# Selective scan and first attention: every third product with b on GpSimd, the second direction's convolution on TensorE, its softplus on GpSimd, and attention values as the stationary operand

## The chip, the cores and the metric

The kernel runs on one core of a Trainium2 chip. It is one launch that holds a whole network of twelve blocks. The metric is the device time in microseconds, lower is better; times are medians of several runs, and each profile is one profiled execution of its own.

## The reference, cut to what matters

The input x has 4 sequences of 128 tokens and 128 channels, the context has 4 sequences of 2048 rows and 96 columns. Twelve blocks are added to x one after the other. The change touches the first two.

The first block is an attention with ternary weights and 8-bit activations. Keys and values are the same projection of the image features, 64 wide and written twice side by side:

```python
for Wa, ba in ((W_att0, b_att0), (W_att1, b_att1)):
    kv = bitnet_linear(image_embeds, Wa, ba)
    k = jnp.concatenate([kv, kv], axis=-1)
    scores = jnp.einsum('bse,bpe->bsp', fused, k) * inv_sqrt_e
    attn = jax.nn.softmax(scores, axis=-1)
    fused = fused + 0.1 * jnp.einsum('bsp,bpe->bse', attn, k)
```

So there are two rounds, each over 4 sequences, 128 queries against 2048 keys.

The second block runs a selective scan over the tokens in both directions and adds the two. For each direction, with 256 inner channels and 16 states:

```python
xc = silu(causal_depthwise_conv4(xi) + conv_b)
delta = softplus(dt @ dtp_w.T + dtp_b)
# for each token t:
dA = jnp.exp(d_t[:, :, None] * A)
h = h * dA + (d_t * u_t)[:, :, None] * b_t[:, None, :]
y = jnp.einsum('bdn,bn->bd', h, c_t)
```

## The kernel before, in words

Tokens of all four sequences lie side by side: 512 columns, and channels lie on the 128 partitions. The code is written as a flow of tile operations, each with its engine named; a framework sets the semaphores and fixes the order of each engine's queue before the run. That order is near the order in the code but not the same: an instruction that is ready is let past one that is not. In the trace the second half of a unit's score matmuls (L959) stands ahead of the transpose o_tr (L996), which the code has first. On the chip each queue is then run in order.

**First attention**, `bit_attention`. A unit is one round and one sequence, so there are eight. The keys kT (L924) and the values v (L931) of a round are in one tile kv; v has 16 chunks of 128 keys for each sequence, 65 wide, and the 65th column is 1 (memset on GpSimd, L910). A unit makes queries (L946 to L949: a matmul with the folding matrix `fold`, a scaling, and the bias added to fused), scores in two groups of 16 matmuls (L959) into PSUM tiles of 1024 columns of which there are three, the maximum over the keys (L961, L964), a transpose, a second maximum, a transpose that spreads it, and a copy (L966 to L973). Then weights: the maximum is subtracted (L977, VectorE) and the exponential taken (L979, ScalarE), one tile p for each group, out of three. Last, values: 32 matmuls (L988) with p as the stationary operand (128 columns) and v as the moving one (65 columns); the 65th output column is the sum of weights. VectorE takes its reciprocal (L992), scales and doubles the 64 columns to 128 (L994), TensorE transposes (L996) and VectorE adds to fused (L997). The values of unit i-1 are written in the code after the weights of unit i. At i = 2 two more ternary weights are made on VectorE (L840, L841, tiles of the tag qtmp, which has two buffers); at i = 3 and 4 half of the context's mask each is loaded by a DMA of SyncE (L1024) into a qtmp tile and turned into floats on GpSimd (L1027).

**Selective scan**, `mamba`. After a layernorm (its square is on GpSimd, L341) `setup(d)` prepares direction d: input projection, a padded copy (L1160 on GpSimd for the zeros, L1161 on ScalarE), the convolution as one product and three fused products and sums on VectorE for each half of the channels (L1165, L1167), silu, projections for dt, b and c, `softplus` for each half (L1084 to L1101, ScalarE for Abs, Exp and Ln, VectorE for the rest), and du (L1205). `setup(0)` runs first; `setup(1)` is a generator that is advanced one step for each state n of direction 0.

Then for each of the 16 states n: b and c are spread over the partitions by a matmul with a one-hot stationary operand (L1210) into PSUM tiles of the tag mm, of which there are three; c is copied to SBUF (cs, L1223, ScalarE), VectorE multiplies du with b (dbu, L1225, 128x1024), and for each half ScalarE takes the exponential dA (L1231, three PSUM tiles in turn) and VectorE runs the scan h (L1234). GpSimd multiplies h with c (hc, L1237, 128x1024) and TensorE adds hc into y with an identity as stationary operand (L1239). The tiles cs, dbu, h and hc have three buffers each. At the end y is gated (L1247, L1249) and projected (L1255).

Both operands of GpSimd's product lie in SBUF, which is what the copy of c is for; b is read by VectorE straight from PSUM.

Of the kernel before, what the change touches and what calls it, by code (L numbers as in the profile page):

```python
# [9 lines left out]
F32 = mybir.dt.float32  # L10
# [4 lines left out]
ALU = mybir.AluOpType  # L15
# [3 lines left out]
P = 128  # L19
B = 4  # L20
T = 128
C = 128
N = B * T
S = 2048
NS = B * S
DC = 96
NCH = S // P
# [233 lines left out]
def bc_mid(ap, n):  # L261

    return ap.unsqueeze(1).to_broadcast([ap.shape[0], n, ap.shape[1]])
# [7 lines left out]
class Net:  # L271
# [534 lines left out]
    def bit_attention(self, nxt):  # L806


        nc, tc = self.nc, self.tc
        w = self.load("l0x")  # L810
        with ExitStack() as es:
            one = es.enter_context(tc.tile_pool(name="bit1", bufs=1))
            wk = es.enter_context(tc.tile_pool(name="bit2", bufs=2))
            big = es.enter_context(tc.tile_pool(name="bit_big", bufs=2))
            BIG = NS // 2 + B * NCH * 65
            qp = es.enter_context(tc.tile_pool(name="bit_q", bufs=1))
            tp = es.enter_context(tc.tile_pool(name="bit_t", bufs=3))

# [30 lines left out]
            ps = es.enter_context(tc.tile_pool(name="bit_ps", bufs=2, space=PSUM))  # L849
# [4 lines left out]
            s, inv = self.absmax([self.ctxT[:DC, b * S : b * S + S] for b in range(B)], "am_ctx")  # L854
# [20 lines left out]
            s, inv = self.absmax(stretches(vis), "am_vis")  # L875
# [3 lines left out]
            total = one.tile([P, NS // W], F32, name="total")  # L879
# [10 lines left out]
            s, inv = self.absmax([xT], "am_x")  # L890
# [11 lines left out]
            fold = one.tile([P, 2, 64], F32, name="fold")  # L902
# [3 lines left out]
            for r, n in enumerate(("att0", "att1")):  # L906
                kv = big.tile([P, BIG], F32, tag="big", name="kv")
                kT = kv[:, 0 : NS // 2]
                v = kv[:, NS // 2 :].rearrange("p (c w) -> p c w", w=65)
                nc.gpsimd.memset(v[:, :, 64:65], 1.0)  # L910
                osc = out_scale(n, s_img)
                osc10 = self.small(1, "osc10" + n)
                nc.vector.tensor_scalar_mul(osc10, osc, 0.1)
                rounds.append((n, kT, v, osc10))
                pairs = qimg.rearrange("p (c h k) -> p c h k", h=2, k=P)
                for j in range(B):
                    mm = stp.tile([P, W], F32, tag="st", name="k_ps")
                    for lo in range(0, W, 512):
                        at = (j * W + lo) // P
                        for h in range(2):  # L920
                            nc.tensor.matmul(
                                mm[h * 64 : h * 64 + 64, lo : lo + 512], qw[:, L0X[n]], pairs[:, at : at + 4, h],
                                start=True, stop=True)
                    nc.scalar.activation(  # L924
                        kT[:, j * W : j * W + W], mm, AF.Identity, bias=self.col("b_" + n), scale=osc)
                    mm = stp.tile([P, W], F32, tag="st", name="v_ps")
                    for i in range(NCH):
                        at = (j * NCH + i) * P
                        nc.tensor.matmul(
                            mm[:, i * 64 : i * 64 + 64], qimg[:, at : at + P], qw[:, L0X[n]], start=True, stop=True)  # L930
                    nc.vector.tensor_copy(  # L931
                        v[:, j * NCH : j * NCH + NCH, 0:64], mm.rearrange("p (c w) -> p c w", w=64))

            class Unit:

# [8 lines left out]
                def queries(u):  # L944
                    mm = ps.tile([P, 512], F32, tag="mm", name="fq_ps")
                    nc.tensor.matmul(mm[:, 0:T], self.flat(fold), u.fb, start=True, stop=True)  # L946
                    u.q = wk.tile([P, T], F32, tag="fq", name="fq")
                    nc.vector.tensor_scalar_mul(u.q, mm[:, 0:T], 1.0 / math.sqrt(C))
                    nc.vector.scalar_tensor_tensor(  # L949
                        u.fb, self.col("b_" + u.n).to_broadcast([P, T]), 0.1, u.fb, ALU.mult, ALU.add)  # L950
                    u.mh = wk.tile([P, 2, P], F32, tag="mh", name="mh")

                def scores(u, g):
                    u.st[g] = stp.tile([P, 2, HC // 2, P], F32, tag="st", name="st")
# [20 lines left out]
                def weights(u, g):  # L975
# [3 lines left out]
                    nc.scalar.activation(p, p, AF.Exp)  # L979
                    u.ts.append(p)  # L980

                def values(u):
                    av = ps.tile([P, 512], F32, tag="mm", name="av")
                    for g in range(2):
                        for h in range(2):
                            for c in range(HC // 2):
                                ch = u.b * NCH + 2 * (g * (HC // 2) + c) + h
                                nc.tensor.matmul(  # L988
                                    av[:, 0:65], u.ts[g][:, h * (HC // 2) + c], u.v[:, ch],
                                    start=g + h + c == 0, stop=g + h == 2 and c == HC // 2 - 1)  # L990
                    r = self.small(1, "rsum")
                    nc.vector.reciprocal(r, av[:, 64:65])  # L992
                    o = wk.tile([P, 2, 64], F32, tag="o", name="o")
                    nc.vector.tensor_scalar(o, bc_mid(av[:, 0:64], 2), r, u.osc10, ALU.mult, ALU.mult)  # L994
                    mm = ps.tile([P, 512], F32, tag="mm", name="o_tr")
                    nc.tensor.transpose(mm[:, 0:P], self.flat(o), self.ident)  # L996
                    nc.vector.tensor_add(u.fb, u.fb, mm[:, 0:P])  # L997

            units = [Unit(r, b) for r in range(2) for b in range(B)]
            units[0].queries()  # L1000
# [80 lines left out]
        nc.gpsimd.memset(self.ctx[:, :, DC : DC + 1], 1.0)  # L1081
        nc.sync.dma_start(self.ctx[:, :, 0:DC], self.A["ctx"].rearrange("(c p) d -> p c d", p=P))

    def softplus(self, pool, out, v, bias, w):  # L1084

        nc = self.nc
        e = pool.tile([P, w], F32, tag="sp_e", name="sp_e")
        nc.scalar.activation(e, v, AF.Abs, bias=bias)  # L1090
        nc.scalar.activation(e, e, AF.Exp, scale=-1.0)
        s = pool.tile([P, w], F32, tag="sp_s", name="sp_s")
        nc.vector.tensor_scalar_add(s, e, 1.0)
        ln = pool.tile([P, w], F32, tag="sp_l", name="sp_l")
        nc.scalar.activation(ln, s, AF.Ln)
        r = pool.tile([P, w], F32, tag="sp_r", name="sp_r")
        nc.vector.tensor_scalar(r, v, bias, 0.0, ALU.add, ALU.max)
        nc.vector.tensor_scalar_add(s, s, -1.0)
        nc.vector.tensor_sub(e, e, s)
        nc.vector.tensor_add(ln, ln, e)  # L1100
        nc.vector.tensor_add(out, r, ln)  # L1101

    def mamba(self, nxt):

# [7 lines left out]
        with ExitStack() as es:  # L1112
# [22 lines left out]
            xn = one.tile([P, B, C], F32, name="xn")  # L1135
            self.layernorm(tp, self.x, xn)
            yT = one.tile([P, 2, 2, N], F32, name="yT")

            def mm_tile(name):
                return ps.tile([P, N], F32, tag="mm", name=name)  # L1140

            def setup(d):
# [12 lines left out]
                for half in range(2):  # L1155
                    i = d * 2 + half
                    mm = mm_tile("xi_ps")
                    nc.tensor.matmul(mm, w[:, at + half * P : at + half * P + P], xT, start=True, stop=True)
                    pad = tp.tile([P, B, T + 3], F32, tag="pad", name="pad")
                    nc.gpsimd.memset(pad[:, :, 0:3], 0.0)  # L1160
                    nc.scalar.copy(pad[:, :, 3:], mm.rearrange("p (b t) -> p b t", b=B))  # L1161
                    yield
                    cw = self.col("conv_w")[:, i * 4 : i * 4 + 4]
                    acc = tp.tile([P, B, T], F32, tag="conv", name="conv")
                    nc.vector.tensor_scalar_mul(acc, pad[:, :, 0:T], cw[:, 0:1])  # L1165
                    for k in range(1, 4):
                        nc.vector.scalar_tensor_tensor(  # L1167
                            acc, pad[:, :, k : k + T], cw[:, k : k + 1], acc, ALU.mult, ALU.add)
                    nc.scalar.activation(
                        u[:, half], self.flat(acc), AF.Silu, bias=self.col("conv_b")[:, i : i + 1])  # L1170
                    yield
# [24 lines left out]
                for half in range(2):  # L1196
                    i = d * 2 + half
                    mm = mm_tile("dt_ps")
                    nc.tensor.matmul(
                        mm, dtp[96:XP, d * 256 + half * P : d * 256 + half * P + P], dt[96:XP],  # L1200
                        start=True, stop=True)
                    self.softplus(tp, delta[:, half], mm, self.col("dtp_b")[:, i : i + 1], N)
                    yield
                du = wk.tile([P, 2, N], F32, tag="du", name="du")
                nc.vector.tensor_mul(du, delta, u)  # L1205
# [9 lines left out]
            for d in range(2):  # L1215
# [3 lines left out]
                for n in range(16):  # L1219
# [2 lines left out]
                    cs = lp.tile([P, N], F32, tag="cs", name="cs")  # L1222
                    nc.scalar.copy(cs, cn)  # L1223
                    dbu = lp.tile([P, 2, N], F32, tag="dbu", name="dbu")
                    nc.vector.tensor_mul(dbu, du, bc_mid(bn, 2))  # L1225
                    h = lp.tile([P, 2, N], F32, tag="h", name="h")
                    for half in range(2):
                        j = (d * 2 + half) * 16 + n
# [741 lines left out]
```

## Time and profile before

| | |
|---|---|
| median of 3 runs | 1679.18 us (1677.23 to 1680.57) |
| the profiled execution | 1656.7 us |
| its span, first to last instruction | 1654.5 us |
| mean granted TensorE clock | 0.824 |
| busy: PE, DVE, ACT, POOL | 1228.3, 999.1, 620.6, 140.9 us |
| first attention's units (window) | 80 to 170 us |
| states of the scan, both directions | 228 to 372.7 us |

PE is TensorE's matmuls and PEld its loads of the stationary operand, DVE is VectorE, ACT is ScalarE, POOL is GpSimd, SP is SyncE. A line of the chain of work gives start, length and what ran; "issue" is time in which the engine waited for nothing that the profile shows. A line of waits reads: who waited, for whom, us in total, times, longest. A line in order of time reads: start, length, engine, line, operation, output<-inputs, shapes, and in brackets how long the engine had been idle and what ended that. A group line reads: count | busy us, mean ns | idle before. Where several instructions are merged (x2), the length is that of all.

### The profile page before, as it was taken

Reading aid. Unit: us, or ns where it says so; the run is one execution under the profiler, and the core shown is the slowest. Engines: PE = TensorE matmul, PEld = TensorE weight load, DVE = VectorE, ACT = ScalarE, POOL = GpSimd, SP = SyncE. Lnnn points to the kernel's source line nnn. Section 1 sums busy time; section 2 is a strip of 40 time slices with the busy share of each in tenths; the row PEclk is TensorE's granted clock in tenths of the full one; section 3 lists DMA queues with packets and bytes.
Section 4 is the critical chain, followed back from the end, with each engine's and each line's share of the span. In section 5 each row is a group of like instructions: output and inputs, shape, how many; then the busy total and the mean of one; then the engine's idle time right before and its main releaser. Section 6 shows DMA issues by size and latency. Waiting matters only on the chain.

```text
span 1654.5 us, 15539 instructions
## 1 busy us (share of the span) xinstructions
PE 1228.3 (74%) x6142; PEld 656.7 (40%) x6142; DVE 999.1 (60%) x1568; ACT 620.6 (38%) x796; POOL 140.9 (9%) x108
## 2 busy tenths in 40 slices
PE   2688456676999999999648054989958148899857
PEld 0377222224444444444213032754426024555534
DVE  8966478993266767667567954124657665444335
ACT  3722255442155655556333001324523102333332
POOL 0010024470000000000002000000020100000000
PEclk9967558798599999999869576978978567899778
DMA  5000000005000000000010004010000000000010
GB/s 158 1 1 1 0 0 26 0 1 161 1 24 1 0 1 1 0 1 1 0 51 1 0 0 127 1 23 19 1 2 1 9 0 1 1 2 1 7 48 7
DMA packets 9371, 28.19 MB, mean 17 GB/s; under 512 B 1175, under 2 KB 7104, under 8 KB 8142
## 3 DMA queue, kind: packets, MB, share of 16 engines
q1 hardware_dynamic: 8174, 24.88, 5.2%
q10 hardware_dynamic: 1120, 2.27, 0.4%
q8 instruction: 50, 0.82, 0.2%
q14 instruction: 27, 0.22, 0.0%
HBM read 26.88 MB, written 0.26 MB: 16 GB/s over the span
## 4 chain that ended last, share of the span: by engine, by line
PE 62%; DVE 25%; ACT 5%; issue 4%; POOL 3%; DMA 1%; POOLq 0%; ACTq 0%; DVEq 0%; SPq 0%
PE sc L495 12%; PE av L529 12%; PE s_ps L673 3%; DVE na_m L678 3%; PE mm L1317 3%; PE t_ps L697 3%; PE q_ps L438 2%; DVE h L1234 2%; PE av L988 2%; PE av L710 2%; PE h_ps L1666 2%; PE y_ps L1673 2%; PE y_ps L1239 2%; POOL hc L1237 1%; PE st L959 1%
## 5 line engine op out<-in xcount | busy, mean ns | idle before, releaser
L495 PE MATMUL sc<-q_aug,ctxT 99*128 99x512 f32 x448 | 213.2, 602 | 1.8 <-DVE q_aug L439 1.8
L529 PE MATMUL av<-s,ctx 128*97 128x512 f32 x448 | 206.8, 597 | 6.6 <-ACT s L527 6.0
L497 ACT COPY s<-sc 128x1024 f32<-128x1024 f32 x112 | 112.9, 1008 | 114.8 <-PE sc L495 114.8
L526 DVE TENSOR_TENSOR s<-s,mbs 128x1024 f32<-128x1024 f32 x112 | 132.4, 1218 | 38.8 <-ACT mbs L521 38.8
L678 DVE TENSOR_REDUCE na_m<-s_ps 128x2 f32<-128x1024 f32 x64 | 75.8, 1221 | 89.8 <-PE s_ps L673 89.6
L527 ACT ACTIVATE s<-s 128x1024 f32<-128x1024 f32 x112 | 115.5, 1056 | 36.0 <-DVE s L526 35.3
L505 DVE TENSOR_TENSOR m<-m,s 128x1024 f32<-128x1024 f32 x72 | 87.9, 1221 | 66.3 <-ACT s L497 66.3
L529 PEld LDWEIGHTS av<-s,ctx 128*97 128x97 f32 x448 | 73.1, 165 | 125.0 <-issue 105.6
L495 PEld LDWEIGHTS sc<-q_aug,ctxT 99*128 99x128 f32 x448 | 82.7, 193 | 93.9 <-issue 82.7
L1239 PE MATMUL y_ps<-hc,consts 128*128 128x512 f32 x128 | 75.3, 723 | 33.6 <-POOL hc L1237 30.7
L703 ACT ACTIVATE p<-t_ps 128x1024 f32<-128x1024 f32 x64 | 62.0, 1021 | 92.5 <-PE t_ps L697 92.5
L1237 POOL TENSOR_TENSOR hc<-h,cs 128x1024 f32<-128x1024 f32 x32 | 77.5, 2433 | 86.3 <-DVE h L1234 86.0
L1234 DVE TENSOR_TENSOR_SCAN h<-dA,dbu 128x512 f32<-128x512 f32 x64 | 74.4, 1202 | 3.6 <-ACT dA L1231 3.4
L341 POOL TENSOR_TENSOR ln_sq<-ln_xc 128x512 f32<-128x512 f32 (+1 forms) x19 | 23.3, 1227 | 503.4 <-DVE ln_xc L339 496.6
L673 PE MATMUL s_ps<-kT,q 32*128 32x512 f32 x256 | 63.7, 711 | 2.1 <-DVE na_m L678 1.1
L697 PE MATMUL t_ps<-q,kT 32*128 32x128 f32 x1024 | 56.3, 329 | 8.8 <-DVE na_m L678 5.8
L1239 PEld LDWEIGHTS y_ps<-hc,consts 128*128 128x128 f32 x128 | 26.0, 222 | 83.2 <-POOL hc L1237 57.0
L697 PEld LDWEIGHTS t_ps<-q,kT 32*128 32x128 f32 x1024 | 46.7, 223 | 27.3 <-DVE na_m L678 16.2
L1231 ACT ACTIVATE dA<-delta,A 128x508 f32<-128x508 f32 x64 | 42.7, 689 | 33.1 <-DVE h L1234 32.1
L358 PE MATMUL tr_xnT<-consts,xn 128*128 128x128 f32 x32 | 8.7, 428 | 60.0 <-DVE xn L348 41.2
L345 ACT ACTIVATE ln_sd<-ln_v,eps 128x4 f32<-128x4 f32 (+1 forms) x19 | 5.7, 300 | 124.5 <-DVE ln_v L343 124.5
L439 DVE TENSOR_SCALAR q_aug<-q_ps,qb 99x512 f32<-99x512 f32 x20 | 15.0, 751 | 46.5 <-PE q_ps L438 46.5
(574 smaller groups left out, 2128.7 us busy)
## 6 DMA issues: line engine op xcount, KB each, us to landing
w_moe<-in_moe SPq DMA_DIRECT2D x2, 2048.0 KB, 8.2
ctxT<-in_ctxT SPq DMA_DIRECT2D x4, 768.0 KB, 12.6
rows<-in_rows ACTq DMA_DIRECT2D x1, 2048.0 KB, 12.4
w_l3f<-in_l3f SPq DMA_DIRECT2D x1, 1920.0 KB, 8.0
w_l0f<-in_l0f SPq DMA_DIRECT2D x1, 1024.0 KB, 4.9
w_mamba<-in_mamba SPq DMA_DIRECT2D x1, 976.0 KB, 19.0
w_r<-in_r SPq DMA_DIRECT2D x1, 960.0 KB
consts<-in_consts SPq DMA_DIRECT2D x1, 832.0 KB, 17.1
```

The source lines that it names most:

```text
L495: nc.tensor.matmul(sc[:, i], self.ctxT[:, at : at + P], u.q, start=True, stop=True)
L497: nc.scalar.copy(s, sc)
L505: nc.vector.tensor_max(u.m, u.m, u.s[j])
L526: nc.vector.tensor_sub(p, p, bc_mid(u.mb, 2))
L527: nc.scalar.activation(p, p, AF.Exp)
L529: nc.tensor.matmul(u.av[: DC + 1], self.ctx[:, u.b * NCH + chunks[2 * j + i]], p[:, i], start=j + i == 0, stop=j == n - 1 and i == 1)
L673: nc.tensor.matmul(ts[g // 2][:, g % 2], qs[lo : lo + 32], kT[lo : lo + 32, s, j * 512 : j * 512 + 512], start=True, stop=True)
L678: nc.vector.tensor_reduce(part[:, at : at + 2], t, axis=AX, op=ALU.max, negate=True)
L697: nc.tensor.matmul(ts[g // 2][:, g % 2, j], kT[g * 32 : g * 32 + 32, s, at : at + P], qs[g * 32 : g * 32 + 32], start=True, stop=True)
L1234: nc.vector.tensor_tensor_scan(h[:, half], self.flat(dA), dbu[:, half], 0.0, ALU.mult, ALU.add)
L1237: nc.gpsimd.tensor_mul(hc, h, bc_mid(cs, 2))
L1239: nc.tensor.matmul(y[:, half], self.ident, hc[:, half], start=n == 0, stop=n == 15)
```

## The change

Every third state's product with b moves to GpSimd, with a copy of b to SBUF on ScalarE. The convolution of the second direction becomes four accumulating matmuls per half with diagonal matrices, which GpSimd makes once from the identity. The five VectorE steps of softplus other than the one that reads PSUM move to GpSimd in the second direction. In the first attention, v becomes the stationary operand (64 columns) and p the moving one (128 columns); even and odd chunks write to the two halves of the output's partitions; the sum of weights is made by three adds on GpSimd for each group and two matmuls with a matrix of ones; the halves are folded by a matmul with `fold`.

```diff
+                half = p[:, 0 : HC // 2]
+                a = wk.tile([P, HC // 2, P], F32, tag="qtmp", name="psum")
+                nc.gpsimd.tensor_add(a, half, p[:, HC // 2 :])
+                nc.gpsimd.tensor_add(a[:, 0:2], a[:, 0:2], a[:, 2:4])
+                nc.gpsimd.tensor_add(u.total[:, g], a[:, 0], a[:, 1])
 def values(u):
     av = ps.tile([P, 512], F32, tag="mm", name="av")
     for g in range(2):
-        for h in range(2):
-            for c in range(HC // 2):
+        for c in range(HC // 2):
+            for h in range(2):
                 ch = u.b * NCH + 2 * (g * (HC // 2) + c) + h
                 nc.tensor.matmul(
-                    av[:, 0:65], u.ts[g][:, h * (HC // 2) + c], u.v[:, ch],
-                    start=g + h + c == 0, stop=g + h == 2 and c == HC // 2 - 1)
-    r = self.small(1, "rsum")
-    nc.vector.reciprocal(r, av[:, 64:65])
-    o = wk.tile([P, 2, 64], F32, tag="o", name="o")
-    nc.vector.tensor_scalar(o, bc_mid(av[:, 0:64], 2), r, u.osc10, ALU.mult, ALU.mult)
-    mm = ps.tile([P, 512], F32, tag="mm", name="o_tr")
-    nc.tensor.transpose(mm[:, 0:P], self.flat(o), self.ident)
-    nc.vector.tensor_add(u.fb, u.fb, mm[:, 0:P])
+                    av[h * 64 : h * 64 + 64, 0:T], u.v[:, ch], u.ts[g][:, h * (HC // 2) + c],
+                    start=g + c == 0, stop=g == 1 and c == HC // 2 - 1)
+    mm = ps.tile([P, 512], F32, tag="mm", name="rsum")
+    for g in range(2):
+        nc.tensor.matmul(mm[:, 0:T], self.ones, u.total[:, g], start=g == 0, stop=g == 1)
+    o = wk.tile([P, T], F32, tag="o", name="o")
+    nc.vector.reciprocal(o, mm[:, 0:T])
+    nc.vector.tensor_mul(o, o, av[:, 0:T])
+    nc.tensor.matmul(mm[:, T : 2 * T], self.flat(fold), o, start=True, stop=True)
+    nc.vector.scalar_tensor_tensor(u.fb, mm[:, T : 2 * T], u.osc10, u.fb, ALU.mult, ALU.add)
...
-    def softplus(self, pool, out, v, bias, w):
+    def softplus(self, pool, out, v, bias, w, eng):
...
-        nc.vector.tensor_scalar_add(s, e, 1.0)
+        eng.tensor_scalar_add(s, e, 1.0)
...
-        nc.vector.tensor_scalar_add(s, s, -1.0)
-        nc.vector.tensor_sub(e, e, s)
-        nc.vector.tensor_add(ln, ln, e)
-        nc.vector.tensor_add(out, r, ln)
+        eng.tensor_scalar_add(s, s, -1.0)
+        eng.tensor_sub(e, e, s)
+        eng.tensor_add(ln, ln, e)
+        eng.tensor_add(out, r, ln)
...
+            diag = one.tile([P, 8, P], F32, name="diag")
+            for j in range(8):
+                nc.gpsimd.tensor_scalar_mul(diag[:, j], self.ident, self.col("conv_w")[:, 8 + j : 9 + j])
...
+                    if d:
+                        acc = mm_tile("conv_ps").rearrange("p (b t) -> p b t", b=B)
+                        for k in range(4):
+                            nc.tensor.matmul(
+                                acc, diag[:, half * 4 + k], pad[:, :, k : k + T], start=k == 0, stop=k == 3)
+                    else:
...
-                    self.softplus(tp, delta[:, half], mm, self.col("dtp_b")[:, i : i + 1], N)
+                    self.softplus(
+                        tp, delta[:, half], mm, self.col("dtp_b")[:, i : i + 1], N, nc.gpsimd if d else nc.vector)
...
-                    nc.vector.tensor_mul(dbu, du, bc_mid(bn, 2))
+                    if n % 3 == 2:
+                        bs = lp.tile([P, N], F32, tag="bs", name="bs", bufs=1)
+                        nc.scalar.copy(bs, bn)
+                        nc.gpsimd.tensor_mul(dbu, du, bc_mid(bs, 2))
+                    else:
+                        nc.vector.tensor_mul(dbu, du, bc_mid(bn, 2))
```

Besides, v loses its 65th column and the memsets that filled it (L910), and each unit gets a tile `total` for the sums.

More of the change, by code (lines that the diff above doesn't have):

```diff
@@ L814, in bit_attention @@
             big = es.enter_context(tc.tile_pool(name="bit_big", bufs=2))
-            BIG = NS // 2 + B * NCH * 65
+            BIG = NS
             qp = es.enter_context(tc.tile_pool(name="bit_q", bufs=1))
@@ L908, in bit_attention @@
                 kT = kv[:, 0 : NS // 2]
-                v = kv[:, NS // 2 :].rearrange("p (c w) -> p c w", w=65)
-                nc.gpsimd.memset(v[:, :, 64:65], 1.0)
+                v = kv[:, NS // 2 :].rearrange("p (c w) -> p c w", w=64)
                 osc = out_scale(n, s_img)
@@ L931, in bit_attention @@
                     nc.vector.tensor_copy(
-                        v[:, j * NCH : j * NCH + NCH, 0:64], mm.rearrange("p (c w) -> p c w", w=64))
+                        v[:, j * NCH : j * NCH + NCH], mm.rearrange("p (c w) -> p c w", w=64))
             class Unit:
@@ L951, in queries @@
                     u.mh = wk.tile([P, 2, P], F32, tag="mh", name="mh")
+                    u.total = wk.tile([P, 2, P], F32, tag="total", name="total")
                 def scores(u, g):
@@ L1163, in setup @@
                     cw = self.col("conv_w")[:, i * 4 : i * 4 + 4]
[L1164 to L1168, printed above, removed]
+                    if d:
[4 more added lines that the diff above has]
+                    else:
+                        acc = tp.tile([P, B, T], F32, tag="conv", name="conv")
+                        nc.vector.tensor_scalar_mul(acc, pad[:, :, 0:T], cw[:, 0:1])
+                        for k in range(1, 4):
+                            nc.vector.scalar_tensor_tensor(
+                                acc, pad[:, :, k : k + T], cw[:, k : k + 1], acc, ALU.mult, ALU.add)
                     nc.scalar.activation(
```

## Prediction

> **What bounds the kernel now.** I read the page's busy tenths and chain first, then the busy time of the two stages that the diff touches, then the chain, the waits and the instructions in order of time inside them. The change lies in the first 382 us; the other 1272 us of the span are the same instructions and I give them no change. By stage (length, busy time of PE, PE loads, DVE, ACT and POOL with counts, granted clock):
>
> ```profile
> 80.00:170.00 90.00, 75.08 (x568) 68.00 (x568) 55.91 (x99) 21.52 (x26) 7.52 (x2) 0.72 0.01 1
> 228.00:372.70 144.70, 99.87 (x211) 36.68 (x210) 133.75 (x128) 73.28 (x112) 77.64 (x33) 0.85 0.02 8
> ```
>
> The scan stretch (228 to 372.7) is bound by DVE: busy 133.75 of 144.7 us, idle 11. POOL works half of it and waits for DVE's scans. In the second direction the chain is DVE alone, 6.72 us for two states n:
>
> ```profile
> 346.53 1.20 DVE dbu L1225 x2
> 347.73 0.97 issue
> 348.86 0.97 issue
> 349.83 1.76 DVE h L1234 x2
> 352.06 1.19 DVE h L1234
> 353.25 1.20 DVE dbu L1225 x2
> ```
>
> The attention (80 to 170) is bound by PE where the clock is low and shared with DVE where it is full. Its waits:
>
> ```profile
> DVE rsum L992 <- PE av L988: 10.1, 5, 5.2
> ACT p L979 <- DVE p L977: 14.3, 9, 1.9
> POOL hc L1237 <- DVE h L1234: 86.0, 23, 26.4
> ACT dA L1231 <- DVE h L1234: 32.1, 22, 3.3
> ```
>
> The last two are of the scan. In time, one unit's value product at the low and one at the full clock, and DVE and POOL together in the scan:
>
> ```profile
> 131.36 6.93 PE L988 MATMUL av<-kv,p 128*128 128x65 f32 x32
> 143.73 3.68 PE L988 MATMUL av<-kv,p 128*128 128x65 f32 x32
> 258.87 2.44 POOL L1237 TENSOR_TENSOR hc<-h,cs 128x1024 f32<-128x1024 f32 x1 [2.95 <-DVE h L1234]
> 259.14 2.72 DVE L1167 SCALAR_TENSOR_TENSOR conv<-pad,cols,conv 128x512 f32<-128x512 f32 x1
> 262.92 0.72 DVE L1167 SCALAR_TENSOR_TENSOR conv<-pad,cols,conv 128x512 f32<-128x512 f32 x1
> ```
>
> The same DVE step takes 2.72 us when a POOL product starts first and 0.72 when POOL is idle.
>
> **What the Trainium skill says.** "SBUF — State Buffer", section "Who interferes with whom": DVE and GpSimd share one pair of ports; a DVE instruction with two SBUF inputs is blocked whole by a GpSimd one that reads SBUF, one with a single SBUF input is not. The trace agrees: 2.72 against 0.72 above, while the scans (one input in PSUM) stay at 1.13 to 1.22 us beside hc. "GPSIMD Engine Reference", section 3.1: an elementwise product of two tensors is 1.96 times slower on GpSimd; here hc takes 2.34 us where dbu, of the same shape, takes 1.16 on DVE: 2.0. "TensorEngine Tiling (Array Packing)", section "When to Use Tiling": with at most 64 columns on the moving side, swap the operands and tile two columns wide. No two-wide 128-row product is in the trace; a four-wide one (L710, 32 matmuls) takes 1.07 us, against 3.68 above. "TensorE: Matmul & The Clock Gate", Part 1: the clock falls to half after idle time; the trace has 0.50 from 102 to 114 us, though PE is 96% busy there, so I don't build on a rule for it.
>
> **The change part by part.**
>
> *Third products (L1225).* n = 2, 5, 8, 11, 14 of each direction, ten in all. Off DVE: 10 x 1.16 = 11.6 us. Onto POOL: 10 x 2.34 (the hc row) = 23.4 us. Onto ACT: ten copies bn to bs at 0.59 (the cs row) = 5.9 us, beside 73 us of work in 145, so hidden; the one bs buffer frees when POOL has done its product. POOL's queue is in order: behind a product stands the next hc, behind that y's matmuls; ahead of it may stand hc of n-1.
>
> *Convolution of direction 2 (L1165, L1167).* Off DVE, with the blocking in them: 1.15+0.72+1.70+0.72 and 0.46+2.72+0.72+0.72 = 8.9 us. Onto PE: 8 matmuls of 128x512, 0.43 us each at full clock, 0.86 at half: 3.4 to 6.9 us. PE is busy 100 of 145 us here, so they are hidden; it takes one of the three mm banks for longer, which I count in the stalls below. The eight diag products on POOL (128x128, one input, no such row; between the 128x128 memset at 0.21 and the 128x128 product at 0.72, so 1.7 to 5.8 us, I take 3.5) come before ln_sq and the pad memset in POOL's queue. POOL is free from 183 to 189, so most is hidden; if they start only with x ready at 185.9, ln_sq, which is on the chain, is late by 0 to 3 us. I take +1.
>
> *Softplus of direction 2 (L1093, L1098 to L1101).* Off DVE: (0.40+0.43+0.67+0.66+1.35) + (0.43+0.40+0.67+1.71+0.66) = 7.4 us. Onto POOL: per half two one-input steps (no row; below the 1.05 of ln_sq on 128x512, above half of it: 0.6) and three at 1.05 = 4.35; 8.7 in all. Its length from input to delta was 8 to 9 us a half on DVE and stays about so; the four states left after setup hide it.
>
> *Sum of the stretch.* DVE 133.75 - 11.6 - 8.9 - 7.4 = 105.9 us. POOL 77.6 + 23.4 + 8.7 = 109.7 us. If nothing is lost, the stretch is 110; if DVE's old idle time stays and POOL costs nothing, 144.7 - 27.9 = 116.8. The unknown is the idle time s that each of the ten POOL products gives to DVE. In steady state POOL has four products in three states, 9.4 us, and DVE 9.2, where it had 3 x 3.36 = 10.1; with three dbu buffers a product can start three states ahead, so s can be near zero; at the worst hc and the product stand one after the other between two scans, 2 x 2.34 + 0.3 = 5. Steps with two SBUF inputs that stay (du, x3, yT, six in all) are blocked for about as long as now. Two engines with equal load cannot both be full: I take s = 1. Stretch 116.8 + 10 = 127, gain 18.
>
> *Attention.* Value product: 32 matmuls now take 3.68 us (115 ns each) at full and 6.93 at half clock, and 3.09+6.73+6.35+6.73+3.52+3.52+5.49 = 35.4 us of them are on the chain. After, 64 columns are loaded for each and 128 stream, in pairs: at best half of a lone 128-column pass (the chain has L495 at 1.72 us for four of 512 columns, 430 ns each; 430/4/2 = 54 ns); at worst the 70 ns of the score pairs (1.16 us for 16, a pair of row halves). I take 62, a ratio of 0.54: -16 us. Two matmuls with ones take 0.3 to 0.5 us more per unit: +3. The reciprocal grows from 128x1 (0.17) to 128x128. The nearest row is
>
> ```profile
> L1368 DVE RECIPROCAL nrm<-nrm 128x512 f32<-128x512 f32 x1 | 3.4, 3352 | 0.0
> ```
>
> so a quarter, 0.84 us; with mul 0.28 for o 0.41 it is +0.54 per unit, on DVE's way between two maxima: +4. The transpose becomes the fold matmul, the add a fused step, same cost. POOL gets three adds per group, 1.05 + 0.84 + 0.70 = 2.6 us, 5.2 per unit in 8 to 12 us: hidden, since values come a unit later. But they run when DVE does mh's max (L964) and the bias step (L949), both with two SBUF inputs and the max on the chain: a block of 0 to 1.05 us, I take 0.4 per unit, +3. The psum tile shares the two qtmp slots with the mask: the mask's DMAs (SP, L1024) wait for a free slot, and behind them on SP the dtp load, needed 80 us later; the mask steps (POOL, L1027, 3.76 us each) stand ahead of the sums of two units: 0 to 3 us, hidden by the unit of slack. The two memsets (L910) were hidden: nothing. Sum -16 + 3 + 4 + 3 = -6, from -13 (no block, no visible reciprocal) to +2 (sums late by 2 to 3 us in two units, PE waiting in order behind).
>
> *Total.* -18 + 1 - 6 = -23 us. The profiled execution took 1656.7 us (span 1654.5 and 2.2 around it), so 1633.7 for such a one; the median of the runs, 1679.18, is 22.5 us above it and the cut is taken off that: 1656.
>
> **The rivals.** With s the time is 1679.2 - 32.9 + 10 s (27.9 and 6 off, 1 on).
>
> *Slower: POOL's product in the scan's path.* If hc(n-1) and then dbu(n) stand between scan n-1 and scan n, s is 5: -32.9 + 50 = +17, 1696 us. It decides from s = 3.3 on. For it: POOL would be 86% busy at 127 us and its order is fixed. Against it: in the trace dbu is made for two states ahead of the scans (1.20 x2, then four h), so the order looks ahead.
>
> *Little gain.* s = 2 and the attention gives nothing (blocks, the reciprocal, clock): -32.9 + 6 + 20 = -7, 1672 us. For it: at full clock a unit is 8.2 us with 6.9 of DVE in it, and DVE gets 0.5 more.
>
> *More gain.* s = 0 and the denser products keep the clock up, so that the low-clock units (12.5 us) go toward 8.2: -33 and some -6 more, 1640 us.
>
> **How the numbers follow.** Forecast 0.58, more gain 0.07, little gain 0.17 (of which 0.07 comes out within 0.2%), slower 0.18. A measurement of this kernel can tell about 0.2%, 3.4 us, from no change. Faster 0.58 + 0.07 + 0.10 = 0.75. The range reaches from just under the best case, 1638, to 1682, where only the slower case is left out.
>
> **What would show it.** Right: the scan stretch at about 127 us with DVE near 106 and POOL near 110 busy; dbu on POOL at 2.3 to 2.5 us; DVE waiting for POOL about 10 us in all; 32 av matmuls in 2.0 us at full clock; a reciprocal of 0.84; mh's max sometimes at 1 us instead of 0.28. Wrong: POOL products longer than 2.6, h waiting for a POOL dbu for over 3 us each, units of attention no shorter than 10 us on average, ln_sq late by more than 3 us, or the stages after 382 us changed in length by more than 5.

## The result and the profile after

The changed kernel takes 1660.89 us (median of 4 runs, 1657.26 to 1665.40), the kernel before beside it 1679.88 us (1677.23 to 1682.20): ratio 0.9889, 95% interval 0.9855 to 0.9923. Ratios here and below leave out executions over 1.5% above the fastest of their kernel, while differences in us are between medians of all, so the two need not agree (in e3 below, 18 and 23 us). The forecast of 1656.0 us was 5 us too low. The sign and the size came out, yet the two terms behind them did not: the scan costs time, and the attention gives far more than its 6 us.

The profiled executions stand the other way round: 1656.7 us before, 1663.99 us after (span 1661.7). The kernel before scatters from 1656 to 1690 us from one execution to the next, and its profile caught a quick one. So I compare stages at fixed marks. The scan's layernorm (ln_sq, L341) starts at 189.42 us before and 184.81 after, the next block's ln_sq at 383.57 and 392.45: the first part is 4.6 us shorter, the scan's block 207.6 instead of 194.2 us. From there to the end it is the same code, 1270.9 and 1269.3 us.

The two stages after the change, as length, busy time of PE, PE loads, DVE, ACT and POOL with counts, and granted clock:

```profile
80.00:163.80 83.80, 61.68 (x627) 50.77 (x627) 66.27 (x104) 22.70 (x28) 46.53 (x50) 0.84 0.01 2
223.30:380.80 157.50, 112.32 (x223) 41.93 (x222) 110.79 (x100) 80.98 (x124) 112.23 (x53) 0.81 0.02 7
```

In the attention the clock is 0.84 instead of 0.72 and TensorE 74% busy instead of 83%. In the scan DVE has 111 us of work instead of 134 and the stretch is 13 us longer: each of DVE and POOL is busy for some 70% of it, and neither alone sets its length. The waits of the scan say where (engine, line, who released it; total, times, longest):

```profile
POOL hc L1261 <- DVE h L1258: 38.5, 16, 6.2
DVE h L1258 <- POOL dbu L1247: 18.8, 9, 4.8
DVE dbu L1249 <- PE b_ps L1229: 13.7, 4, 8.5
DVE du L1224 <- POOL delta L1109: 3.5, 1, 3.5
DVE sp_r L1105 <- POOL delta L1109: 3.3, 1, 3.3
```

The first was there before (86.0 us then). The other four are 39 us in which DVE stands; with the old scan the third is 1.8 us (e3 below) and the rest are not there. The chain in the second direction, which was DVE alone, now runs in this order (pieces under 0.1 us left out):

```profile
343.68 2.35 POOL hc L1261
346.03 2.32 POOL dbu L1247
348.41 1.10 issue
349.51 1.21 DVE h L1258
350.88 2.11 POOL hc L1261
352.99 0.20 issue
353.19 2.35 POOL hc L1261
355.54 2.32 POOL dbu L1247
357.88 1.23 DVE h L1258
```

Two hc, one dbu, and only then the next scan: POOL's product does not start ahead, it is queued behind hc of the states just scanned. The price of the instructions was not the fault:

```profile
L1247 POOL TENSOR_TENSOR dbu<-du,bs 128x1024 f32<-128x1024 f32 x10 | 24.0, 2400 | 23.4 <-DVE du L1224 21.8 <-ACT bs L1246 1.6
L1101 POOL TENSOR_SCALAR sp_s<-sp_e 128x512 f32<-128x512 f32 x2 | 3.2, 1582 | 0.0
L1107 POOL TENSOR_TENSOR sp_e<-sp_e,sp_s 128x512 f32<-128x512 f32 x2 | 2.5, 1266 | 0.2
```

dbu is 2.40 us, as forecast. The steps of softplus are dearer than forecast (1.58 and 1.27 against 0.6 and 1.05). In the attention, one unit's value product, and the reciprocal and the maximum on DVE:

```profile
136.17 1.97 PE L995 MATMUL av<-p,kv 128*64 128x128 f32 x32
```

```profile
L1002 DVE RECIPROCAL o<-rsum 128x128 f32<-128x128 f32 x8 | 7.6, 952 | 5.0 <-PE rsum L1000 5.0
L964 DVE TENSOR_TENSOR mh<-mh 128x128 f32<-128x128 f32 x8 | 4.2, 521 | 0.1
```

The 1.97 us are the 62 ns per matmul of the forecast; the reciprocal takes 0.95 (forecast 0.84); the maximum 0.52 on average, 0.285 before. These 62 ns are for one record of the trace, which has two for each value matmul of the code: the x32 are the 16 value matmuls of a unit. The score matmuls and those of the convolution have two records each as well.

### The profile page after: what moved, and what is told of

It reads as the page before. It is cut to its first block, busy times and chain, and to the rows that moved or that the text cites. A ratio compares the mean times of both kernels' runs of the same rounds, so it can differ in the third digit from the quotient of the medians.

```text
span 1661.7 us, 15727 instructions
## 1 busy us (share of the span) xinstructions
PE 1229.6 (74%) x6198; PEld 645.5 (39%) x6198; DVE 985.0 (59%) x1540; ACT 628.5 (38%) x808; POOL 217.5 (13%) x182
## 4 chain that ended last, share of the span: by engine, by line
PE 61%; DVE 23%; POOL 6%; ACT 5%; issue 4%; DMA 1%; POOLq 0%; ACTq 0%; DVEq 0%
PE sc L495 12%; PE av L529 12%; PE s_ps L673 4%; DVE na_m L678 3%; PE mm L1341 3%; PE t_ps L697 3%; PE q_ps L438 2%; POOL hc L1261 2%; PE h_ps L1690 2%; PE av L710 2%; PE y_ps L1697 2%; PE y_ps L1263 2%; DVE h L1258 2%; PE o_ps L1762 1%; POOL ln_sq L341 1%
## 5 line engine op out<-in xcount | busy, mean ns | idle before, releaser
L1263 PE MATMUL y_ps<-hc,consts 128*128 128x512 f32 x128 | 81.5, 785 | 34.4 <-POOL hc L1261 33.7
L703 ACT ACTIVATE p<-t_ps 128x1024 f32<-128x1024 f32 x64 | 62.0, 1021 | 91.4 <-PE t_ps L697 91.3
L341 POOL TENSOR_TENSOR ln_sq<-ln_xc 128x512 f32<-128x512 f32 (+1 forms) x19 | 23.3, 1226 | 496.0 <-DVE ln_xc L339 496.0
L1258 DVE TENSOR_TENSOR_SCAN h<-dA,dbu 128x512 f32<-128x512 f32 x64 | 74.3, 1207 | 21.3 <-POOL dbu L1247 18.8
## 6 DMA issues: line engine op xcount, KB each, us to landing
rows<-in_rows ACTq DMA_DIRECT2D x1, 2048.0 KB, 13.2
```

What stands on the lines that cost most here:

```text
L1258: nc.vector.tensor_tensor_scan(h[:, half], self.flat(dA), dbu[:, half], 0.0, ALU.mult, ALU.add)
L1263: nc.tensor.matmul(y[:, half], self.ident, hc[:, half], start=n == 0, stop=n == 15)
```

## The experiments

The theory that these runs came to test: the attention gives all of the gain, and by TensorE's clock rather than by its work; the scan's edits cost some 13 us, because POOL's queue holds the next scan back. The clock came into it only after the first four runs, whose expectations do not know of it. The rivals: the scan gains as forecast and the attention little; within the scan, that POOL's load or the convolution's place in TensorE's queue is what costs; for the clock, that it falls by chance.

### The two kernels again, and each half of the change alone

**e1_before_again**: no edit.

> The kernel before, unchanged. Its first profiled execution took 1656.7 us while its timed runs took 1677 to 1682. If the 23 us between them is a property of single executions, this profile and these times should scatter over both values; if it is a property of the chip or of the day, the profile taken here should agree with the times taken here within 0.3%, and its stages should tell where the 23 us lie. In the stages that the diff touches I expect the same lengths as in the first profile: attention units to about 170 us, scan stretch 144.6 us.

Measured: 1678.15 us (1658.38 to 1689.55), ratio to the kernel before 1.0009 (0.9960 to 1.0058).

**e2_after_again**: no edit.

> The changed kernel, unchanged. By its first profile the x of the scan is ready 9 us later than in the first profile of before (390.0 against 381.0 us): attention 7 us shorter, scan stretch 157.5 instead of 144.6 us. Theory A (the profiles compare like with like): about 7 us slower than before on the same chip. Theory B (the prediction: DVE's load decides): 19 to 23 us faster, and the scan stretch is then not what the profile shows.

Measured: 1661.51 us (1657.24 to 1669.72), ratio 0.9927 (0.9905 to 0.9949).

**e3_attention_alone**: `bit_attention` from the change, the scan from the kernel before.

> Only the attention with stationary values; the scan as before. Prediction's term: 6 us faster. By the first profile of the changed kernel: 7 us faster (last values done at 163.6 instead of 170.5 us).

Measured: 1653.02 us (1649.94 to 1660.70), ratio 0.9891 (0.9842 to 0.9939).

**e4_scan_alone**: the other way round.

> Only the three edits of the scan; the attention as before. Prediction's term: 17 us faster, with the scan stretch at about 127 us. By the first profile of the changed kernel (chain hc, then dbu on POOL, then h): scan stretch about 157 us and 13 us slower than before.

Measured: 1691.68 us (1687.38 to 1694.64), ratio 1.0108 (1.0060 to 1.0155).

What follows: the attention alone is 23 us faster than the kernel before (1675.8 us beside it), the scan's edits alone are 16 us slower. e3 is far beyond the 6 to 7 us that were expected, and e2 met neither of its theories: it is 14 us faster, with the long scan of the first profile. The marks give the cost of the scan more exactly, since the same code after them took 1267 to 1280 us in these profiles. The block from ln_sq to ln_sq: 194.2 and 194.8 us in the two profiles of the kernel before and 194.4 in e3, 207.6 and 207.8 in the two of the change, 205.2 in e4. The scan's edits cost 11 to 13 us in their own block. The first part, to the scan's ln_sq: 184.8, 184.2 and 183.3 us with the new attention; 189.4, 211.0 and 211.9 with the old one. So most of the scatter of the kernel before is the old attention's: of the 31 us between its two profiles 22 lie there and 9 in the code after the scan. That a middling execution, of which there is no profile, is slow for the same reason is likely and not shown.

With it goes the clock. Old attention (e4, then the first profile of the kernel before), then the new one (e3); the fields are those of the stages above:

```profile
90.00:100.00 10.00, 10.00 (x65) 9.77 (x63) 3.73 (x6) 1.86 (x3) 0.00 (x0) 0.50 0.00 0
...
120.00:140.00 20.00, 17.50 (x94) 15.53 (x93) 11.59 (x18) 2.68 (x5) 7.51 (x2) 0.50 0.01 3
140.00:160.00 20.00, 19.11 (x107) 17.69 (x106) 8.28 (x14) 4.46 (x5) 0.00 (x0) 0.50 0.00 1
```

```profile
120.00:140.00 20.00, 17.50 (x99) 15.90 (x98) 9.31 (x15) 4.76 (x6) 7.22 (x2) 0.50 0.01 1
140.00:160.00 20.00, 16.31 (x157) 14.35 (x155) 14.66 (x26) 4.95 (x7) 0.00 (x0) 0.98 0.00 1
```

```profile
120.00:140.00 20.00, 15.01 (x148) 12.53 (x148) 16.02 (x24) 5.33 (x7) 17.98 (x15) 0.83 0.01 3
140.00:160.00 20.00, 14.48 (x152) 11.92 (x152) 13.40 (x24) 4.76 (x6) 13.41 (x17) 0.91 0.00 1
```

In e4 the clock is 0.50 while TensorE is 88 to 100% busy. The first profile of the kernel before left this low clock at about 140 us; e4 kept it to the attention's end, and so did the profile of e1 (1687.8 us, among the longest executions of its kernel). The new attention is less busy and gets 0.83 and 0.91.

### Is it the clock? The old attention with more columns

**e8_old_attention_wide_values**: the kernel before, the value products stream each chunk twice.

```diff
-    av[:, 0:65], u.ts[g][:, h * (HC // 2) + c], u.v[:, ch],
+    av[:, 0:130].rearrange("p (i w) -> p i w", i=2),
+    u.ts[g][:, h * (HC // 2) + c], bc_mid(u.v[:, ch], 2),
```

> The kernel before, with one edit: the value products stream the same 65 columns twice (130 moving columns, results of the second copy unused). TensorE gets more work and no operation is taken away. Clock theory (with 128 columns loaded for 65 streamed, the loads hold the products back, and the granted clock stays at 0.5 through the attention; with 130 columns streamed per load it is granted 0.8 or more): attention ends at 163 to 172 us instead of 192, time 1650 to 1662. Rival (the low clock comes by chance or from the other work of the attention, not from the load-bound products): the clock stays at 0.5 in 100 to 160 us, the products get longer by up to 2 us each at half clock, and the time is 1676 to 1690.

Measured: 1655.61 us (1650.38 to 1658.97), ratio 0.9883 (0.9826 to 0.9939). The attention's last unit ends at 164.6 us (162.6 in e3, 192.8 in e4).

```profile
120.00:140.00 20.00, 15.23 (x122) 13.15 (x122) 14.12 (x23) 4.76 (x6) 5.30 (x2) 0.83 0.00 1
140.00:160.00 20.00, 16.05 (x147) 14.23 (x147) 14.29 (x27) 6.87 (x8) 0.00 (x0) 1.00 0.00 1
```

```profile
147.10 3.74 PE L988 MATMUL av<-kv,p 128*128 128x130 f32 x32
```

What follows: useless columns added to the old products, nothing taken away, and the kernel is 22.6 us faster than the one before beside it (1678.2). The columns are free at the same clock: 3.74 us for 32 records against 3.68 with 65. With half the columns loaded and as many streamed, e12 below takes 2.57, so the pace goes with the loads and not with the columns streamed. The rival, chance, is out: of 105 timed executions of the kernel before in these sessions 16 took under 1663 us, of e8 all five did. The reciprocal, the ones matmuls and POOL's sums of the change are not needed for this gain. What exactly the throttle counts these runs do not show.

**e12_halves_not_alternated**: the new attention alone, the two column halves one after the other within each group of weights.

```diff
-    for c in range(HC // 2):
-        for h in range(2):
+    for h in range(2):
+        for c in range(HC // 2):
```

> The new attention alone with one edit: the value products of one column half come all before those of the other, instead of taking turns. Pair theory (two products on different column halves run at once): 32 of them take 3.5 us or more instead of 1.97, the attention ends 5 to 12 us later than the 162.6 us of the new attention alone, time 1658 to 1665. Rival (the gain is in the shorter load of 64 columns, and turns between halves give nothing): 2.0 to 2.3 us, attention's end and time within 2 us of the new attention alone, 1653. If the clock falls to 0.5, the attention ends at 175 us or later in either case.

Measured: 1654.82 us (1649.15 to 1657.06), ratio 0.9882 (0.9835 to 0.9929); attention's end at 162.0 us.

```profile
134.95 2.57 PE L995 MATMUL av<-p,kv 128*64 128x128 f32 x32
```

Both missed: 2.57 us lie between the two forecasts. Alternating the halves gives 80 to 62 ns for each record, not half. The 0.6 us per unit do not show in the attention's end (162.6 in e3); as e12 also had the higher clock from 140 to 160 us (1.00 against 0.91), that they hide behind DVE is not shown. The swap of the operands gives the larger step, from 115 to 80.

### The scan's three edits one at a time, on the new attention

No profile of the new attention falls to the low clock of e4, so the block can be read against e3's 194.4 us. The five profiles with the old scan, e8 and e12 among them, lie between 194.2 and 194.8.

**e5_dbu_on_new_attention**: e3 with the third products on GpSimd.

```diff
+    if n % 3 == 2:
+        bs = lp.tile([P, N], F32, tag="bs", name="bs", bufs=1)
+        nc.scalar.copy(bs, bn)
+        nc.gpsimd.tensor_mul(dbu, du, bc_mid(bs, 2))
```

> The new attention plus the third products on GpSimd alone, convolution and softplus as before. The clock of the new attention is steady, so the time is to be read against the new attention alone (1653.0 us) and the block from the scan's ln_sq to the grouped FFN's ln_sq against its 194.4 us. Theory (queue order on GpSimd: the product of b stands behind the hc of earlier states, and the scan waits for it): h waits for a GpSimd dbu by some 15 to 19 us in total, more than the 11.6 us taken off VectorE; block about 200 us, time about 1659. Rival (the loss comes from the convolution and the softplus, which hold banks and GpSimd during setup): h waits under 8 us, block 190 or less, time 1649 or less.

Measured: 1667.92 us (1660.54 to 1672.32), ratio 0.9948 (0.9929 to 0.9967); block 208.2 us.

**e6_conv_on_new_attention**: e3 with the second direction's convolution on TensorE (and the diag products).

```diff
+    if d:
+        acc = mm_tile("conv_ps").rearrange("p (b t) -> p b t", b=B)
+        for k in range(4):
+            nc.tensor.matmul(
+                acc, diag[:, half * 4 + k], pad[:, :, k : k + T], start=k == 0, stop=k == 3)
```

> The new attention plus the second direction's convolution on TensorE alone. Theory (conv_ps holds one of the three banks until silu has read it, and the spread of b for the coming states waits behind it on TensorE): dbu waits for b_ps by some 10 us more than in the new attention alone, against 8.9 us taken off VectorE: block 194 to 198 us, time 1653 to 1657. Rival (the wait for b_ps in the changed kernel came only together with the other two parts): block 187 or less, time 1646 or less.

Measured: 1657.66 us (1654.37 to 1662.37), ratio 0.9898 (0.9849 to 0.9947); block 199.8 us.

**e7_softplus_on_new_attention**: e3 with the second direction's softplus on GpSimd.

```diff
-    tp, delta[:, half], mm, self.col("dtp_b")[:, i : i + 1], N, nc.vector)
+    tp, delta[:, half], mm, self.col("dtp_b")[:, i : i + 1], N, nc.gpsimd if d else nc.vector)
```

> The new attention plus the second direction's softplus on GpSimd alone. Theory: VectorE loses 7.4 us of work, GpSimd gets about 2 x 7.0 us (two steps of 1.55 and three of 1.28) in the middle of the scan's last states of the first direction, where hc is late by it, and delta is late by 3 to 7 us: block 193 to 197 us, time 1652 to 1656. Rival (softplus on GpSimd is hidden by the states left and VectorE's 7.4 us are gained): block 188 or less, time 1647 or less.

Measured: 1652.99 us (1651.15 to 1654.90), ratio 0.9868 (0.9813 to 0.9922); block 195.0 us.

The waits of DVE over the block, in e5, e6 and e7:

```profile
DVE h L1254 <- POOL dbu L1243: 10.5, 4, 3.8
DVE dt L1199 <- PE xdbl_ps L1195: 9.6, 2, 6.7
DVE yd L1267 <- PE y_ps L1259: 7.0, 1, 7.0
...
DVE dbu L1245 <- PE b_ps L1225: 5.1, 3, 2.9
```

```profile
DVE dbu L1249 <- PE b_ps L1229: 15.4, 3, 7.9
```

```profile
DVE sp_r L1105 <- POOL delta L1109: 3.6, 1, 3.6
...
DVE du L1220 <- POOL delta L1109: 2.4, 1, 2.4
```

What follows: the third products alone cost 13.8 us, the convolution 5.4, softplus 0.6. That is 19.8 in sum against 13.2 for all three in the change, so the single costs do not add up. e5 and e6 are dearer than both of their forecasts, e7 is as its theory says. In e5 h waits only 10.5 us for POOL and not the 15 to 19 expected; late hc also makes y late on TensorE, and what stands behind y: dt waits 9.6 us for its projection xdbl_ps (4.7 in e3), dbu 5.1 for b (1.8). Nor does DVE lose 11.6 us of work, but 6.8 (159.7 to 152.8 busy over the block), since its other steps get longer beside GpSimd. The convolution takes 8.0 us off DVE and makes it wait 15.4 for b (e3 has 1.8) while the spread of b stands behind conv_ps on TensorE. Softplus is even.

### Place or load on GpSimd

**e9_early_products**: e5, but each product is emitted two states ahead, into two buffers of its own and with a second one for bs. The steps that then use it are left out here.

```diff
-    if n % 3 == 2:
-        bs = lp.tile([P, N], F32, tag="bs", name="bs", bufs=1)
-        nc.scalar.copy(bs, bn)
-        nc.gpsimd.tensor_mul(dbu, du, bc_mid(bs, 2))
+    if n + 2 < 16 and n % 3 == 0:
+        bn = spread(x3, n + 2, "b_ps")
+        bs = lp.tile([P, N], F32, tag="bs", name="bs", bufs=2)
+        nc.scalar.copy(bs, bn)
+        early[n + 2] = lp.tile([P, 2, N], F32, tag="dbp", name="dbp", bufs=2)
+        nc.gpsimd.tensor_mul(early[n + 2], du, bc_mid(bs, 2))
```

> The new attention plus the third products on GpSimd as in e5, but each is emitted two states earlier (spread of b, copy and product of state n+2 ahead of the hc of state n), with two buffers of their own. The block from the scan's ln_sq to the next ln_sq was 194.4 us without GpSimd products and 208.2 in e5. Theory (place in GpSimd's queue: a product just behind hc of n-1 makes the scan of n, then hc of n, y and the next spreads late): h waits for a GpSimd product under 4 us in total, block 186 to 196 us, time 1645 to 1655. Rival (GpSimd's load: ten products of 2.4 us make hc late wherever they stand, and TensorE's y and the spreads behind it late): block 203 us or more, time 1662 or more.

Measured: 1652.74 us (1651.28 to 1655.18), ratio 0.9873 (0.9821 to 0.9925); block 196.6 us.

**e10_four_early_products**: e9 with four products.

```diff
-    if n + 2 < 16 and n % 3 == 0:
+    if n + 2 < 16 and n % 6 == 3:
```

> As e9, but only four products in all (states 5 and 11 of each direction) go to GpSimd, 4.6 us off VectorE. Place theory: block 189 to 192 us, time 1648 to 1651, the best so far. Load theory: GpSimd has 9.6 us more instead of 23.9, and the block is 0.4 of the loss of e5: 197 to 201 us, time 1656 to 1660.

Measured: 1661.51 us (1657.99 to 1668.88), ratio 0.9925 (0.9902 to 0.9948); block 201.5 us.

**e11_four_late_products**: e5 with four products.

```diff
-    if n % 3 == 2:
+    if n % 6 == 5:
```

> As e5, the products where the change has them, but four instead of ten (states 5 and 11 of each direction). Place theory: each costs about what it did in e5 (13.8 us for ten): block 198 to 201 us, time 1656 to 1660. Load theory with a limit (GpSimd has room for four, not for ten): block 189 to 193 us, time 1648 to 1652, as e10.

Measured: 1663.59 us (1658.31 to 1666.12), ratio 0.9944 (0.9918 to 0.9969); block 203.9 us.

What follows: with the same ten products, but earlier in the queue and with more buffers, 11.6 of the 13.8 us are back, and no wait of h for POOL is left. So the load of ten products is not by itself what cost e5 its time. Whether the place or the added buffers (which e10 has too) brought it back, no run takes apart. And e9 gains nothing against e3: DVE has 6.8 us less to do in it, as in e5, yet waits 10.3 us for b (1.8 in e3). Its chain in the second direction (pieces under 0.1 us left out):

```profile
326.93 2.33 POOL hc L1263
329.27 0.25 issue
329.56 1.84 POOL dbp L1241
331.40 0.46 issue
331.86 2.36 POOL hc L1263
334.27 5.40 PE y_ps L1265 x8
339.67 0.23 PE c_ps L1225
339.98 0.58 ACT cs L1246
```

A loop over three queues: hc waits for cs, cs for the spread of c, that spread stands behind y's matmuls on TensorE, and those wait for hc. A product in POOL's queue lengthens this loop wherever it stands; that is my reading of the chain, and no run took the loop apart. I split the block: from the first dbu to du of the second direction, and from there to its first yd (us).

| run | first | second |
|---|---|---|
| e3, no product on POOL | 72.4 | 74.4 |
| e5, ten, as in the change | 81.6 | 77.7 |
| e6, convolution on TensorE | 77.3 | 74.5 |
| e7, softplus on GpSimd | 69.1 | 77.9 |
| e9, ten, early | 73.8 | 72.9 |
| e10, four, early | 79.8 | 74.2 |
| e11, four, as in the change | 79.2 | 75.9 |
| all of the change | 73.6 | 86.9 |

In the second direction, with the scan alone, the order of e3, e5, e9, e10 and e11 is that of the place theory, and e9's early products gain 1.5 us. In the first, where the other direction's setup runs in between, it fails: ten early products cost 1.4 us and four early ones 7.4, as much as four late ones. e9 came out just above the place theory's range, e10 far from its 189 to 192 us and just above the load theory's 197 to 201, e11 above both of its forecasts; why e10 loses there was not settled.

The last row shows where the change itself loses. In the first direction 21 us of DVE's work are gone (65.3 to 44.0 us busy) and the stretch is not shorter; in the second it is 12.5 us longer, where e5, e6 and e7 lose 3.3, 0.1 and 3.5. There h waits 12.5 us for POOL's dbu, in six waits, against 8.3 in three in e5. So most of e5's loss lies in the first direction and most of the change's in the second. That POOL's queue holds the change back is read from its chain and waits; no run moves the products ahead in the whole change.

## Why the prediction was right, and where not

**The scan, −18: wrong, +13.** The loads were right: DVE 110.8 (forecast 105.9), POOL 112.2 (109.7), dbu 2.40. The step that failed is "Two engines with equal load cannot both be full: I take s = 1". By the forecast's own sum, the stretch is 116.8 + 10 s; it measured 157.5, so s = 4.1, past the 3.3 from which "slower" decides. In the change s also holds the waits of the other two edits: h waits 18.8 us for POOL's dbu, 1.9 for each product. The reason given against it, that dbu is made two states ahead, holds for DVE's queue; on POOL the product stood behind hc, as the chain after the change shows. A small misreading besides: dbu on DVE is 1.20 us in the trace before, not 1.16, and hc 2.43 on average, not 2.34. I asked how much work each engine has, not what stands ahead of each product in POOL's order.

**Convolution, hidden: wrong by place.** TensorE had room, but the spread of b for the scan stands behind conv_ps (15.4 us in e6). It was also undercounted: its 8 matmuls are 16 records, 7.4 us busy where 3.4 to 6.9 were forecast. **Softplus: wrong by price and by what it gives.** A half is 6.9 us (1.58 + 1.50 + 3 x 1.27), not 4.35. The 7.4 us off DVE were counted as gained, and e7 is +0.6: delta comes late, and du, said to be held up for about as long as before, takes 3.35 us beside GpSimd in the second direction instead of 1.19. **diag: +1 forecast, +0.4 measured**: of the eight products, 0.61 us each, one stands ahead of ln_sq and seven behind it; DVE waits 2.85 us for ln_sq, 2.41 before.

**The attention against its own profile, −6: right in number, not in cause.** Its end (the start of L777) moved from 170.69 to 163.81 us, 6.9. But e8, which takes no operation away, ends at 164.59. So 6.1 us come with the clock even against this quick profile, and the forecast's terms, which do not count on another clock, net to about 1 or 2 us. Of the terms, av at 62 ns (1.97 us) came as priced, the reciprocal nearly (0.95 for 0.84); the blocked maximum and bias step are 0.24 and 0.21 us longer per unit, 0.44 for a forecast of 0.4. The matmuls with ones take 0.71 us at full clock (four records), not 0.3 to 0.5.

**The total: the step that failed is "the median of the runs, 1679.18, is 22.5 us above it and the cut is taken off that".** It treats those 22.5 us as a constant. As far as the profiles show, they are the old attention at half clock, which the change removes: its end is at 192.8 us in e4 and 162.6 in e3. So the attention is worth 23 us against the median and 7 against the profiled execution. "More gain" named this mechanism with 6 us and a chance of 0.07; "slower" named the scan's, at s = 5. Both happened, −23 and +13, and that the total came near the forecast is luck. They do not even add up to it: −10 by these two, −19 measured (−14 in e2). The times of e2 and e3 differ by 8.5 us only: in their profiles the block is 13.4 us longer in e2, but the code after it, the same in both, 6.2 us shorter, and why is open. For the profiled execution the forecast was 1633.7; it became 1663.99.

**On what the Trainium skill says.** "TensorE: Matmul & The Clock Gate", Part 1, has the clock halved after idle time and released by activity. The runs disagree for this kind of activity: in e4 TensorE is busy for all of 90 to 100 us and stays at 0.50, and more columns on the same loads raise it (e8). "TensorEngine Tiling (Array Packing)", section "When to Use Tiling", agrees in direction: swapped and two columns wide, a record is 62 ns instead of 115, of which alternating is 18. "GPSIMD Engine Reference", section 3.1, gives a ratio of 1.96 for an add of 2048 columns; the product of 1024 columns here is close to it, 2.40 against 1.21 us on DVE.

## What to carry to other kernels

When a kernel scatters by more than a change is worth, find the stage that scatters before adding a cut from one profile to a median: here it was the stage with 128-column loads for 65 streamed columns, and columns added at no cost cured it. Before work moves to an engine with room, write down what will stand ahead of it in that engine's queue, and who waits behind it; in e9 an earlier place, with more buffers, made the same ten products cost 2 us instead of 14, and e10 shows that it is no sure remedy. Of all versions run, the attention alone (1653.0 us) is below the whole change (1661.5 beside it); e7, e8, e9 and e12 do not differ from it by more than these runs can tell.

## What was not expected of the hardware

- TensorE at 0.50 of its clock from 90 to 190 us, 91.4 of these 100 us busy (e4); with 130 instead of 65 columns per load, 0.74 to 1.00 from 90 us to 160, near the attention's end (e8).
- A product of 130 columns on a 128-column fp32 load costs nearly the same as one of 65: 3.74 and 3.68 us for 32 records.
- On GpSimd the one-input step is the slower one: in softplus 128x512 takes 1.50 to 1.58 us, with two inputs 1.27.
- A DVE step with one SBUF input can be held up by GpSimd too: sp_s (L1101) takes 2.14 us at 291.45 us of e5, beside an hc, and 0.40 to 0.43 in its other three executions there.
